# A transformer block on one core: another order of the Down products and another pipeline of the attention's scores

## The chip, the core and the metric

The kernel runs on one core of a Trainium2 chip. The metric is the time of one launch in microseconds on the device. Five engines work side by side and meet at semaphores: TensorE (PE: matmuls, and PEld: its weight loads), VectorE (DVE), ScalarE (ACT), GpSimd (POOL) and SyncE (SP), whose queue issues nearly all transfers. Each engine takes its instructions strictly in the order in which they stand in its own queue.

## The reference

The input x is 4 x 1024 x 512. It goes through a layer norm, and the result `xn` into two branches that are added to x:

```python
h = rmsnorm(xn, qkv_norm_w)
q, k, v = h @ ternary(qkv_w).T          # 16 heads of 32
# linear attention with decay, in chunks of 128 rows; S is a 32x32 state per head
scores = einsum('bhtd,bhsd,hts->bhts', qi, ki, mask)
intra  = einsum('bhts,bhsd->bhtd', scores, vi)
cross  = einsum('bhtd,ht,bhde->bhte', qi, lam_t, S)
o      = scale * (intra + cross)
S      = lam_T * S + einsum('bhtd,ht,bhte->bhde', ki, lam_rev, vi)
out    = rmsnorm(o, norm_w, 1e-06)
att    = rmsnorm(out, proj_norm_w, eps) @ ternary(proj_w).T
ffn    = (silu(xn @ w_gate.T) * (xn @ w_up.T)) @ w_down.T     # hidden 2048
y      = x + att + ffn
```

## The kernel before, in words

**Numbers.** Every float32 operand is split into a high and a low float16 part, and a product is made of two or three float16 products in the same PSUM bank. A split costs an ACT copy (high part) and a subtraction on DVE or POOL (low part).

**Blocks and steps.** The 4096 rows are taken in eight blocks of 512. The FFN of a block is a Python generator; each `yield` of it is one step, and the main loop advances the attention by one step of its own between two FFN steps. So PE's order is: one FFN piece (12 matmuls of 512 columns, or 24 of 256), one attention piece, one FFN piece, and so on. PE's order is the program's (`keep_in_program_order`). A planner with a cost model orders the other engines and the SP queue when the kernel is built, and gives out the buffers of the pools; what it decided stands fixed in each queue.

**FFN.** `ffn_up` makes for hidden tile j the gate product (ACT takes its silu, L716, to `sl`) and the up product (DVE multiplies, L719, to `gf`). From block 2 on, `summed` (L736) takes tiles in pairs: POOL forms differences and sums of their halves (L753 for an even j; L758, L759 and L762 for an odd one), and `split` (L742) splits them: "a" tiles 0 and 1 from the even j, "a" tiles 2 and 3 from the odd j, three "s" tiles from both. The low parts of "a" are POOL's, but for the last pair of a half, where they are DVE's (L746). After eight j, `ffn_seven` (L802) does Down with seven products instead of eight, each a sum over the four pairs, in the order of `SEVEN` (L787), with three PSUM banks. Each entry of `SEVEN` names the tile, the weight row, the bank, whether it begins the bank anew, and the quarters of the output to which DVE then adds the bank (L817). `down_sums` (L824) makes the sums of Down's weights that the seven products need, once, in blocks 1 and 2; their work tile is `ss`, one buffer, which `summed` uses too.

**Attention.** `att_half(b, half)` takes 256 rows, two chunks `u0` and `u1` of 128. There are sixteen such halves; `at` (L986) holds the step at which each starts, 21.5 steps apart in the middle and 14 apart for the last three. Its steps are: q and k in four groups of 16 matmuls of 256 columns (L491), v (L517), two empty steps, then for each chunk four times `scores` and `intra` (four heads each), `cross`, `state`, `norms`, `turn`, `proj`.

- `scores`: 4 matmuls into a bank of `ps_s` (two banks); DVE multiplies with the mask in place (L558), ACT copies the high part (L560), DVE subtracts to the low part (L561).
- `intra`: 8 matmuls with those two as weights. It stands two attention steps after its `scores`, since the two chunks alternate.
- `cross`: 16 matmuls with the state, DVE multiplies to `oc` (L585), POOL adds it to `o` (L586).
- `state`: 12 matmuls; POOL multiplies S with its decay (L598), DVE adds the product in four pieces (L605), ACT and DVE make three float16 copies.
- `norms`: squares on ACT (L616, L619), a product on POOL (L618), nine small DVE operations (L623 to L633) and two POOL powers (L627, L632) for both chunks together; then `o3` on DVE (L636), its split on ACT and POOL (L639, L640), and a transposing DMA (L642).
- `proj`: 8 matmuls on the transposed tiles; DVE adds to the output (L850).

q, k, v, `intra`, `cross`, `state` and `proj` share the three banks of `ps_a`. The buffers that matter are `t32` (512 float32 columns, eight buffers) and `t16` (eleven). In the last half no DMA transposes: `turn` does it on PE (L652) and the two chunks' norms stand apart (`last_half`).

Of the kernel before, what the change touches and what calls it, by code (L numbers as in the profile page):

```python
# [10 lines left out]
F16 = mybir.dt.float16  # L11
# [6 lines left out]
P = 128  # L18
# [10 lines left out]
def block_kernel(ctx, tc, x, qkv_w, qkv_nwT, proj_w, proj_nwT, proj_nw, norm_w, s, w_gu, w_down, out):  # L29
# [95 lines left out]
    def t32():  # L125
        return wt([P, 512], F32, "t32", 8)

# [343 lines left out]
    def att_half(b, half):  # L471
        _, h, rs = blk[b]
        hhi, hlo = h[:, 0], h[:, 1]
        g0 = b * 4 + half * 2
        last_half = g0 == B * N // P - 2

# [35 lines left out]
        for k in range(2):  # L512
# [22 lines left out]
            else:  # L535
                vrs.append(None)
            yield
        class Chunk:
            pass

        cs = []
        for k in range(2):
            u = Chunk()
            u.kn, u.vr = kn[:, :, :, k, :], vrs[k]
            u.g = g0 + k
            u.first = u.g % (N // P) == 0
# [4 lines left out]
            u.pa = None  # L551
            cs.append(u)

        def scores(u, qd):
            pss = bank(ps_s, (P, 4, P))
            for hq in range(4):
                T.matmul(pss[:, hq, :], kst[: 3 * D, hq, qd, u.tsl], qst[: 3 * D, hq, qd, u.tsl], start=True, stop=True)
            V.scalar_tensor_tensor(pss, pss, u.rk, mask[:, 4 * qd : 4 * qd + 4, :], ALU.mult, ALU.mult)  # L558
            u.smh, u.sml = v3(t16()), v3(t16())
            A.copy(u.smh, pss)  # L560
            V.tensor_tensor(u.sml, pss, u.smh, ALU.subtract)  # L561

        def intra(u, qd):
            if qd == 0:
                u.o = t32()
            if qd % 2 == 0:
                u.pa = bank(ps_a, (P, 8, 2, D))
            for hq in range(4):
                h = 4 * qd + hq
                pa = u.pa[:, h % 8].rearrange("p a d -> p (a d)")  # L570
                T.matmul(pa, u.smh[:, hq, :], u.vhl[:, h].rearrange("p a d -> p (a d)"), start=True, stop=False)
                T.matmul(pa[:, :D], u.sml[:, hq, :], u.vhl[:, h, 0, :], start=False, stop=True)
            if qd % 2:
                oh = u.o.rearrange("p (h d) -> p h d", d=D)[:, 4 * qd - 4 : 4 * qd + 4, :]
                A.copy(oh, u.pa[:, :, 1, :])
                V.tensor_tensor(oh, u.pa[:, :, 0, :], oh, ALU.add)  # L576

        def cross(u):
            if u.first:
                return  # L580
            px = bank(ps_a, (P, H, D))
            for h in range(H):
                T.matmul(px[:, h, :], qst[: 3 * D, h % 4, h // 4, u.tsl], Sst[:, h, :], start=True, stop=True)
            oc = t32()
            V.tensor_tensor(oc.rearrange("p (h d) -> p h d", d=D), px, lamt, ALU.mult)  # L585
            G.tensor_tensor(u.o, u.o, oc, ALU.add)  # L586

# [21 lines left out]

        def norms(us):  # L610
            n = len(us)
            k0 = half * 2 + us[0].g - g0
            sq = wt([P, 2, n], F32, f"sq{n}")
            o2s = []
            for i, u in enumerate(us):
                A.activation(junk, u.o, AF.Square, accum_out=sq[:, 0, i : i + 1])  # L616
                o2 = t32()
                G.tensor_tensor(o2, u.o, nw_bc, ALU.mult)  # L618
                A.activation(junk, o2, AF.Square, accum_out=sq[:, 1, i : i + 1])  # L619
                o2s.append(o2)  # L620
            f = wt([P, 4, n], F32, f"f{n}")
            c1, r, r2, e = (f[:, i, :] for i in range(4))
# [11 lines left out]
            for i, u in enumerate(us):  # L634
                u.o3 = t32()
                V.scalar_tensor_tensor(u.o3, o2s[i], e[:, i : i + 1], pnw_bc, ALU.mult, ALU.mult)  # L636
                if u.g < B * N // P - 2:
                    on = wt([P, 2 * C], F16, "vhl", 5).rearrange("p (a c) -> p a c", a=2)
                    A.copy(on[:, 0, :], u.o3)  # L639
                    G.tensor_tensor(on[:, 1, :], u.o3, on[:, 0, :], ALU.subtract)  # L640
                    oT = wt([P, 2 * C], F16, "vhl", 5).rearrange("p (a c t) -> p a c t", a=2, t=P)
                    SY.dma_start_transpose(  # L642
                        oT.rearrange("p a c t -> p (a c) t"), on.rearrange("p a c -> p (a c)")
                    )
                    u.oh, u.ol = oT[:, 0], oT[:, 1]

# [10 lines left out]
        def proj(u):  # L657
# [4 lines left out]
            add_acc(u.g, pp, spp)  # L662

        u0, u1 = cs
        yield
        yield
        scores(u0, 0)
        yield
        scores(u1, 0)
        yield  # L670
        for qd in range(1, 4):
            for u in cs:
                intra(u, qd - 1)
                scores(u, qd)
                yield
        intra(u0, 3)
        cross(u0)
        if last_half:
            norms([u0])
        yield  # L680
        intra(u1, 3)
        yield
        state(u0)
        yield
        yield
        cross(u1)
        norms([u1] if last_half else cs)
        turn(u0)
        yield
        if not u1.last:  # L690
            state(u1)
        yield
        if last_half:
            proj(u0)
        yield
        yield
        turn(u1)
        yield
        if not last_half:
            proj(u0)  # L700
        yield
# [34 lines left out]
    def summed(ops, late):  # L736
# [11 lines left out]
        def done(j, gf):  # L748
# [6 lines left out]
            else:  # L755
                ss = wt([P, 2 * C], F32, "ss", 1)
                f0 = g0[0]
                G.tensor_tensor(ss[:, :UT], gf[:, UT:], f0[:, UT:], ALU.subtract)  # L758
                G.tensor_tensor(ss[:, UT : 2 * UT], ss[:, :UT], f0[:, :UT], ALU.add)  # L759
                split(ops[-1][0][:, 2:], gf, E)  # L760
                split(ops[-1][1][:, :2], ss[:, : 2 * UT], V)
                G.tensor_tensor(ss[:, 2 * UT : 3 * UT], gf[:, :UT], ss[:, :UT], ALU.subtract)  # L762
                split(ops[-1][1][:, 2:3], ss[:, 2 * UT : 3 * UT], V)

        return done

    def ffn_down(b, k, g0, gts, c):
# [56 lines left out]
    def down_sums(g):  # L824

        hh, i = divmod(g, NG // 2)
        w = wt([P, 2, 2, UT], F32, "ss", 1)
        SY.dma_start(w, w_down[2 * g * P : 2 * g * P + 2 * P, :].rearrange("(r p) (f q) -> p r f q", p=P, q=UT))
        for (r, f), (ra, fa), (rb, fb) in (
# [4 lines left out]
        ):  # L834
            G.tensor_tensor(w[:, r, f, :], w[:, ra, fa, :], w[:, rb, fb, :], ALU.subtract)
        o = om[:, g, 2:3]
        for r in range(2):
            t = wt([P, 2 * C], F16, "xn2", 2).rearrange("p (f n q) -> p f n q", f=2, n=2)
            A.activation(t[:, :, 0, :], w[:, r], AF.Copy, scale=o)
            V.scalar_tensor_tensor(t[:, :, 1, :], w[:, r], o, t[:, :, 0, :], ALU.mult, ALU.subtract)  # L840
            SY.dma_start(wd_d[:, hh, 3 + 2 * r : 5 + 2 * r, i].rearrange("p f n q -> p f (n q)"), t.rearrange("p f n q -> p f (n q)"))
# [16 lines left out]
    def load_acc(b):  # L858
        for k in range(2):
            g = 4 * b + 2 * k  # L860
            acc[g // 2] = wt([P, 2, C], F32, "acc", 4)
            SY.dma_start(acc[g // 2], xf[g * P : (g + 2) * P, :].rearrange("(n p) c -> p n c", p=P))
            parts[g] = parts[g + 1] = 1 + (NG if b == 0 else 2 if b == 1 else 8)

# [128 lines left out]
    for b in range(NB):  # L993
        lns = iter(())
        TS = steps[b]
        for i, _ in enumerate(ffn(b) if b else ffn0()):
# [15 lines left out]
            if t == 6 * NG - 6:  # L1012
                SY.dma_start(pnw_bc, proj_nw.partition_broadcast(P))
            if b + 1 < NB:
                if i == TS - (22 if b else 15):
# [62 lines left out]
```

## Time and profile before

| | |
|---|---|
| median of 3 runs | 1374.3 us (1371.63 to 1375.47) |
| profiled execution, its own time | 1374.05 us |
| its span, first to last instruction | 1372.3 us |
| mean granted TensorE clock | 0.989 |
| PE busy | 1306.0 us (95%), 9378 matmuls |
| DVE busy | 893.9 us (65%) |
| ACT busy | 610.2 us (44%) |
| POOL busy | 641.8 us (47%) |
| largest group: gate and up products (L74 psf<-xT,gu), 3072 matmuls | 705.0 us |

How to read the lines. "A <- B: 6.8, 3, 2.9" in the view of waits says that engine line A sat idle 6.8 us in total, 3 times, at most 2.9 us, until B ended. In the timeline a row is a start, a duration, an engine, a source line, the operation, output<-input, shapes and a count; a bracket at its end is the idle time ahead of it and what ended that. PEclk is the share of full TensorE clock that the throttle granted. All matmul helpers have the line L74, so PE's work is told apart by its tiles: psf is the FFN, psa and pss the attention.

### The profile page before, as it was taken

The numbers are of one execution on the slowest core, as the hardware profiler recorded it, in microseconds if no ns is written. First come the engines' busy times: TensorE is split into PE (matmuls) and PEld (weight loads), VectorE is DVE, ScalarE is ACT, GpSimd is POOL, SyncE is SP. The second block draws the span as 40 slices with busy tenths as digits, with TensorE's granted clock in tenths as the row PEclk, the third lists the DMA queues.
The fourth block names the chain that finished last, engine by engine and source line by source line (L and its number), as shares of the span: only waits on it lengthen the run. The fifth ranks groups of instructions, "written<-read, shape, count | busy, mean of one in ns | idle before, by whom it ended". The sixth has DMA issues, their size and how long they took to land.

```text
span 1372.3 us, 23971 instructions
## 1 busy us (share of the span) xinstructions
PE 1306.0 (95%) x9378; PEld 782.9 (57%) x9378; DVE 893.9 (65%) x1599; ACT 610.2 (44%) x1173; POOL 641.8 (47%) x681
## 2 busy tenths in 40 slices
PE   5998999999998999999999999999999999997997
PEld 2443445455556565575757657475665757555645
DVE  7797776654657577665767466575656666557575
ACT  6764554343443435434443354443444254343352
POOL 3757646241453545535463355444554345343352
PEclk9999999999999999999999999999999999998999
DMA  9845756438376583847774656747573747645432
GB/s 342 317 142 169 216 164 205 118 94 215 122 193 212 141 238 99 224 124 201 199 183 142 169 141 187 196 137 208 137 214 117 191 148 164 190 126 137 142 73 77
DMA packets 180689, 233.84 MB, mean 170 GB/s; under 512 B 103264, under 2 KB 113504, under 8 KB 180576
## 3 DMA queue, kind: packets, MB, share of 16 engines
q1 hardware_dynamic: 180432, 232.31, 59.1%
q8 instruction: 73, 1.20, 0.4%
q14 instruction: 40, 0.33, 0.1%
q10 hardware_dynamic: 144, 0.01, 0.0%
HBM read 167.78 MB, written 40.89 MB: 152 GB/s over the span
## 4 chain that ended last, share of the span: by engine, by line
PE 65%; DVE 12%; DMA 10%; POOL 7%; ACT 4%; issue 3%; SPq 1%; POOLq 0%; ACTq 0%; DVEq 0%
PE psf L74 48%; PE psa L74 15%; DMA xin<-in_x_dram 3%; DMA xT<-xn 2%; PE pss L74 2%; DMA vhl<-vhl 1%; DVE t L719 1%; DMA ss<-in_w_down_dram 1%; DVE wda L746 1%; DVE st L396 1%; POOL xn L450 1%; DMA wd_d<-xn 1%; DVE pss L558 1%; DVE t L561 1%; DVE Sst L607 1%
## 5 line engine op out<-in xcount | busy, mean ns | idle before, releaser
L74 PE MATMUL psf<-xT,gu 128*128 128x512 f16 x3072 | 705.0, 382 | 12.5 <-POOL gu L367 4.9
L74 PEld LDWEIGHTS <-gu 128*128 128x128 f16 x3072 | 295.9, 98 | 342.9 <-issue 16.1
L74 PE MATMUL psf<-wdb,ghl 128*128 128x256 f16 (+1 forms) x1344 | 184.4, 294 | 15.3 <-ACT ghl L745 6.8
L74 PEld LDWEIGHTS <-ghl 128*128 128x128 f16 x1536 | 150.4, 100 | 75.1 <-ACT ghl L745 7.7
L560 ACT CAST t<-pss 128x512 f16<-128x512 f32 x128 | 74.7, 585 | 123.0 <-DVE pss L558 121.8
L719 DVE SCALAR_TENSOR_TENSOR t<-psf,bsc,t 128x512 f32<-128x512 f32 x128 | 95.3, 747 | 51.1 <-PE psf L74 36.5
L74 PE MATMUL psa<-h,wqkT 128*128 128x256 f16 x1024 | 122.2, 273 | 1.6 <-DVE t L585 1.6
L716 ACT ACTIVATE t<-psf,ug 128x512 f32<-128x512 f32 x128 | 87.6, 684 | 69.3 <-PE psf L74 68.9
L561 DVE TENSOR_TENSOR t<-pss,t 128x512 f16<-128x512 f32 x128 | 87.9, 687 | 41.5 <-ACT t L560 41.2
L74 PEld LDWEIGHTS <-wqkT 128*128 128x128 f16 x1024 | 99.6, 98 | 21.6 <-issue 1.8
L558 DVE SCALAR_TENSOR_TENSOR pss<-pss,rs,mask 128x512 f32<-128x512 f32 x128 | 96.1, 751 | 14.5 <-PE pss L74 14.1
L745 ACT CAST ghl<-t 128x512 f16<-128x512 f32 x96 | 59.2, 618 | 96.8 <-DVE t L719 55.6
L74 PE MATMUL psf<-wdb,wda 128*128 128x256 f16 x864 | 100.0, 272 | 0.1
L746 DVE TENSOR_TENSOR wda<-ss,wda 128x512 f16<-128x512 f32 x96 | 75.0, 805 | 32.7 <-ACT wda L745 32.0
L533 POOL TENSOR_TENSOR t<-t,t 128x512 f16<-128x512 f32 x28 | 32.8, 1172 | 135.6 <-ACT t L532 135.5
L746 POOL TENSOR_TENSOR ghl<-t,ghl 128x512 f16<-128x512 f32 x72 | 84.2, 1171 | 23.5 <-ACT ghl L745 23.5
L74 PEld LDWEIGHTS <-wda 128*128 128x128 f16 x864 | 83.4, 98 | 9.8 <-issue 0.3
L817 DVE SCALAR_TENSOR_TENSOR acc<-psf,c,acc 128x512 f32<-128x512 f32 x96 | 70.3, 743 | 27.6 <-PE psf L74 27.1
L758 POOL TENSOR_TENSOR ss<-t,t 128x256 f32<-128x256 f32 x48 | 35.8, 746 | 109.8 <-DVE t L719 108.7
L586 POOL TENSOR_TENSOR t<-t,t 128x512 f32<-128x512 f32 x28 | 37.7, 1345 | 90.0 <-DVE t L576 75.3
L753 POOL TENSOR_TENSOR t<-t 128x256 f32<-128x256 f32 x48 | 36.3, 756 | 92.8 <-DVE t L719 92.8
L74 PEld LDWEIGHTS <-t 128*128 128x128 f16 x1040 | 47.7, 97 | 33.1 <-DVE t L561 6.8
(210 smaller groups left out, 1825.2 us busy)
## 6 DMA issues: line engine op xcount, KB each, us to landing
gu<-gu_d SPq DMA_DIRECT2D x112, 512.0 KB, 3.7
wdb<-wd_d SPq DMA_DIRECT2D x84, 512.0 KB, 3.9
qst<-sd SPq DMA_DIRECT2D x48, 256.0 KB, 5.3
kst<-sd SPq DMA_DIRECT2D x48, 256.0 KB, 4.6
xin<-in_x_dram SPq DMA_DIRECT2D x32, 256.0 KB, 4.3
acc<-in_x_dram SPq DMA_DIRECT2D x16, 512.0 KB, 3.9
gu_d<-gu SPq DMA_DIRECT2D x16, 512.0 KB, 4.5
sd<-qhl SPq DMA_DIRECT2D x16, 512.0 KB, 3.1
```

The lines of the kernel that those rows point to most:

```text
L74: tc.keep_in_program_order(nc.tensor.matmul(*a, **k))
L558: V.scalar_tensor_tensor(pss, pss, u.rk, mask[:, 4 * qd : 4 * qd + 4, :], ALU.mult, ALU.mult)
L560: A.copy(u.smh, pss)
L561: V.tensor_tensor(u.sml, pss, u.smh, ALU.subtract)
L586: G.tensor_tensor(u.o, u.o, oc, ALU.add)
L716: pa = A.activation(sl, pm, AF.Silu, scale=ug[:, j // 2 : j // 2 + 1])
L719: pv = V.scalar_tensor_tensor(gf, pm, bs[:, j // 2 : j // 2 + 1], sl, ALU.mult, ALU.mult)
L745: A.copy(dst[:, :, 0, :], src)
L746: E.tensor_tensor(dst[:, :, 1, :], src, dst[:, :, 0, :], ALU.subtract)
L753: G.tensor_tensor(gf[:, UT:], gf[:, :UT], gf[:, UT:], ALU.subtract)
L758: G.tensor_tensor(ss[:, :UT], gf[:, UT:], f0[:, UT:], ALU.subtract)
L817: V.scalar_tensor_tensor(a, pd, c, a, ALU.mult, ALU.add)
```

## The change

It has two parts.

1. `SEVEN` has a new order: the two tiles of the even j first (a0, a1), then those of the odd j (a2, a3), then s1, s0, s2. Tile s0 now adds to three quarters instead of one, and a1 to one instead of two: nine additions on DVE a half instead of eight.
2. The attention: `scores` stands four steps ahead of its `intra`. The masked scores go to a `t32` tile in SBUF, so that the bank is free after one DVE operation, and the low part is POOL's. `cross(u0)` and `state(u0)` stand at the first two score steps, `cross(u1)` and `state(u1)` at the ninth and tenth; `oc` is kept and added to `o` on POOL after the last `intra`. `norms` takes one chunk, and does both norms with one power: four small DVE operations a half (`ek`) and, for each chunk, two additions and a power on POOL replace the nine DVE operations and two powers. A half ends sooner; `at` goes from 21.5 to 21.1 steps. `t32` has ten buffers; `ss` is gone, `down_sums` uses two `t32` tiles, and `summed` uses `xn2` (two buffers, shared with the layer norm).

```diff
     def t32():
-        return wt([P, 512], F32, "t32", 8)
+        return wt([P, 512], F32, "t32", 10)
...
+        ek = wt([P, 2], F32, "ek")
+        V.tensor_scalar(ek, rs[:, 1, half * 2 : half * 2 + 2], kap, None, ALU.mult)
+        V.reciprocal(ek, ek)
+        V.tensor_scalar(ek, ek, (1e-6 * RMS_EPS) ** 0.5, 1e18, ALU.mult, ALU.min)
+        V.tensor_tensor(ek, ek, ek, ALU.mult)
...
         def scores(u, qd):
...
-            V.scalar_tensor_tensor(pss, pss, u.rk, mask[:, 4 * qd : 4 * qd + 4, :], ALU.mult, ALU.mult)
-            u.smh, u.sml = v3(t16()), v3(t16())
-            A.copy(u.smh, pss)
-            V.tensor_tensor(u.sml, pss, u.smh, ALU.subtract)
+            sm = v3(t32())
+            V.scalar_tensor_tensor(sm, pss, u.rk, mask[:, 4 * qd : 4 * qd + 4, :], ALU.mult, ALU.mult)
+            smh, sml = u.sm[qd] = v3(t16()), v3(t16())
+            A.copy(smh, sm)
+            G.tensor_tensor(sml, sm, smh, ALU.subtract)
...
         def intra(u, qd):
...
+            if qd == 3 and not u.first:
+                G.tensor_tensor(u.o, u.o, u.oc, ALU.add)
 
         def cross(u):
...
-            oc = t32()
-            V.tensor_tensor(oc.rearrange("p (h d) -> p h d", d=D), px, lamt, ALU.mult)
-            G.tensor_tensor(u.o, u.o, oc, ALU.add)
+            u.oc = t32()
+            V.tensor_tensor(u.oc.rearrange("p (h d) -> p h d", d=D), px, lamt, ALU.mult)
...
-        def norms(us):
...
-            V.tensor_scalar(c1, rs[:, 1, k0 : k0 + n], kap, None, ALU.mult)
-            V.tensor_tensor(e, c1, c1, ALU.mult)
-            V.tensor_tensor(r, sq[:, 0, :], e, ALU.mult)
-            V.tensor_scalar(r, r, 1.0 / C, 1e-6, ALU.mult, ALU.add)
-            G.tensor_tensor(r, r, mhalf[:, :n], ALU.pow)
-            V.tensor_tensor(r, r, c1, ALU.mult)
-            V.tensor_tensor(e, r, r, ALU.mult)
-            V.tensor_tensor(r2, sq[:, 1, :], e, ALU.mult)
-            V.tensor_scalar(r2, r2, 1.0 / C, RMS_EPS, ALU.mult, ALU.add)
-            G.tensor_tensor(r2, r2, mhalf[:, :n], ALU.pow)
-            V.scalar_tensor_tensor(e, r2, ps_sc, r, ALU.mult, ALU.mult)
...
+        def norms(u):
...
+            A.activation(junk, o, AF.Square, scale=(RMS_EPS / C) ** 0.5, accum_out=sq[:, 0:1])
+            o2 = t32()
+            G.tensor_tensor(o2, o, nw_bc, ALU.mult)
+            A.activation(junk, o2, AF.Square, scale=(1.0 / C) ** 0.5, accum_out=sq[:, 1:2])
+            f = sq[:, 2:3]
+            G.tensor_tensor(f, sq[:, 0:1], u.ek, ALU.add)
+            G.tensor_tensor(f, f, sq[:, 1:2], ALU.add)
+            G.tensor_tensor(f, f, mhalf[:, :1], ALU.pow)
+            u.o3 = t32()
+            V.scalar_tensor_tensor(u.o3, o2, f, pnw_bc, ALU.mult, ALU.mult)
...
+        order = [(u, qd) for qd in range(4) for u in cs]
+        yield
+        yield
+        for i in range(len(order) + 4):
+            if i >= 4:
+                intra(*order[i - 4])
+            if i < len(order):
+                scores(*order[i])
+            if i in (0, 8):
+                cross(cs[i // 8])
+            if i in (1, 9) and not cs[i // 8].last:
+                state(cs[i // 8])
+            if i >= 10:
+                norms(cs[i - 10])
+            yield
+        yield
         turn(u0)
         yield
...
         turn(u1)
         yield
-        if not last_half:
-            proj(u0)
+        proj(u0)
         yield
         proj(u1)
...
-                ss = wt([P, 2 * C], F32, "ss", 1)
+                ss = wt([P, C], F32, "xn2", 2)
...
+                split(ops[-1][1][:, :2], ss, V)
+                s4 = wt([P, C], F32, "xn2", 2)[:, :UT]
+                G.tensor_tensor(s4, gf[:, :UT], ss[:, :UT], ALU.subtract)
+                split(ops[-1][1][:, 2:3], s4, V)
...
     SEVEN = (
         (("a", 0), 0, 1, True, ((0, 0),)),
-        (("a", 3), 5, 0, True, ((1, 0),)),
+        (("a", 1), 4, 0, True, ((1, 1),)),
         (("a", 2), 1, 2, True, ((0, 0),)),
-        (("s", 0), 6, 1, False, ((0, 1),)),
+        (("a", 3), 5, 0, False, ((1, 0),)),
         (("s", 1), 3, 2, True, ((1, 1),)),
-        (("a", 1), 4, 1, False, ((1, 1), (1, 0))),
+        (("s", 0), 6, 1, False, ((0, 1), (1, 0), (1, 1))),
         (("s", 2), 2, 2, False, ((0, 1),)),
     )
...
     def down_sums(g):
...
-        w = wt([P, 2, 2, UT], F32, "ss", 1)
+        w = [t32(), t32()]
...
-    at = [round(36 + 22.4 * min(n, 4) + 21.5 * max(n - 4, 0)) for n in range(2 * NB - 2)]
+    at = [round(36 + 22.4 * min(n, 4) + 21.1 * max(n - 4, 0)) for n in range(2 * NB - 2)]
```

More of the change, by code (lines that the diff above doesn't have):

```diff
@@ L474, in att_half @@
         g0 = b * 4 + half * 2
-        last_half = g0 == B * N // P - 2
         qst = wt([P, 4, CC, UT], F16, "qst", 1)
@@ L550, in att_half @@
             u.rk = rs[:, 1, half * 2 + k : half * 2 + k + 1]
-            u.pa = None
+            u.ek = ek[:, k : k + 1]
+            u.pa, u.sm = None, {}
             cs.append(u)
@@ L567, in intra @@
                 u.pa = bank(ps_a, (P, 8, 2, D))
+            smh, sml = u.sm.pop(qd)
             for hq in range(4):
@@ L570, in intra @@
                 pa = u.pa[:, h % 8].rearrange("p a d -> p (a d)")
-                T.matmul(pa, u.smh[:, hq, :], u.vhl[:, h].rearrange("p a d -> p (a d)"), start=True, stop=False)
-                T.matmul(pa[:, :D], u.sml[:, hq, :], u.vhl[:, h, 0, :], start=False, stop=True)
+                T.matmul(pa, smh[:, hq, :], u.vhl[:, h].rearrange("p a d -> p (a d)"), start=True, stop=False)
+                T.matmul(pa[:, :D], sml[:, hq, :], u.vhl[:, h, 0, :], start=False, stop=True)
             if qd % 2:
@@ L608, in state @@
             A.activation(Sst[D : 2 * D], S, AF.Copy, scale=STS / VS)
-        def norms(us):
[L611 to L622, printed above, removed]
-            V.tensor_scalar(c1, rs[:, 1, k0 : k0 + n], kap, None, ALU.mult)
-            V.tensor_tensor(e, c1, c1, ALU.mult)
-            V.tensor_tensor(r, sq[:, 0, :], e, ALU.mult)
-            V.tensor_scalar(r, r, 1.0 / C, 1e-6, ALU.mult, ALU.add)
-            G.tensor_tensor(r, r, mhalf[:, :n], ALU.pow)
-            V.tensor_tensor(r, r, c1, ALU.mult)
-            V.tensor_tensor(e, r, r, ALU.mult)
-            V.tensor_tensor(r2, sq[:, 1, :], e, ALU.mult)
-            V.tensor_scalar(r2, r2, 1.0 / C, RMS_EPS, ALU.mult, ALU.add)
-            G.tensor_tensor(r2, r2, mhalf[:, :n], ALU.pow)
-            V.scalar_tensor_tensor(e, r2, ps_sc, r, ALU.mult, ALU.mult)
[L634 to L645, printed above, removed]
@@ new lines, in norms @@
+        def norms(u):
+            o = u.o
+            sq = wt([P, 3], F32, "sq")
+            A.activation(junk, o, AF.Square, scale=(RMS_EPS / C) ** 0.5, accum_out=sq[:, 0:1])
[8 more added lines that the diff above has]
+            V.scalar_tensor_tensor(u.o3, o2, f, pnw_bc, ALU.mult, ALU.mult)
+            if u.g < B * N // P - 2:
+                on = wt([P, 2 * C], F16, "vhl", 5).rearrange("p (a c) -> p a c", a=2)
+                A.copy(on[:, 0, :], u.o3)
+                G.tensor_tensor(on[:, 1, :], u.o3, on[:, 0, :], ALU.subtract)
+                oT = wt([P, 2 * C], F16, "vhl", 5).rearrange("p (a c t) -> p a c t", a=2, t=P)
+                SY.dma_start_transpose(
+                    oT.rearrange("p a c t -> p (a c) t"), on.rearrange("p a c -> p (a c)")
+                )
+                u.oh, u.ol = oT[:, 0], oT[:, 1]
@@ L664, in att_half @@
         u0, u1 = cs
+        order = [(u, qd) for qd in range(4) for u in cs]
         yield
         yield
-        scores(u0, 0)
-        yield
[L669 to L687, printed above, removed]
-        turn(u0)
[L689 to L693, printed above, removed]
-            proj(u0)
-        yield
+        for i in range(len(order) + 4):
[10 more added lines that the diff above has]
+            yield
+        yield
+        turn(u0)
         yield
@@ L698, in att_half @@
         yield
-        if not last_half:
-            proj(u0)
+        proj(u0)
         yield
@@ L826, in down_sums @@
         hh, i = divmod(g, NG // 2)
-        w = wt([P, 2, 2, UT], F32, "ss", 1)
-        SY.dma_start(w, w_down[2 * g * P : 2 * g * P + 2 * P, :].rearrange("(r p) (f q) -> p r f q", p=P, q=UT))
+        w = [t32(), t32()]
+        for r in range(2):
+            SY.dma_start(w[r], w_down[(2 * g + r) * P : (2 * g + r + 1) * P, :])
+        w = [t.rearrange("p (f q) -> p f q", q=UT) for t in w]
         for (r, f), (ra, fa), (rb, fb) in (
@@ L834, in down_sums @@
         ):
-            G.tensor_tensor(w[:, r, f, :], w[:, ra, fa, :], w[:, rb, fb, :], ALU.subtract)
+            G.tensor_tensor(w[r][:, f, :], w[ra][:, fa, :], w[rb][:, fb, :], ALU.subtract)
         o = om[:, g, 2:3]
@@ L838, in down_sums @@
             t = wt([P, 2 * C], F16, "xn2", 2).rearrange("p (f n q) -> p f n q", f=2, n=2)
-            A.activation(t[:, :, 0, :], w[:, r], AF.Copy, scale=o)
-            V.scalar_tensor_tensor(t[:, :, 1, :], w[:, r], o, t[:, :, 0, :], ALU.mult, ALU.subtract)
+            A.activation(t[:, :, 0, :], w[r], AF.Copy, scale=o)
+            V.scalar_tensor_tensor(t[:, :, 1, :], w[r], o, t[:, :, 0, :], ALU.mult, ALU.subtract)
             SY.dma_start(wd_d[:, hh, 3 + 2 * r : 5 + 2 * r, i].rearrange("p f n q -> p f (n q)"), t.rearrange("p f n q -> p f (n q)"))
@@ L862, in load_acc @@
             SY.dma_start(acc[g // 2], xf[g * P : (g + 2) * P, :].rearrange("(n p) c -> p n c", p=P))
-            parts[g] = parts[g + 1] = 1 + (NG if b == 0 else 2 if b == 1 else 8)
+            parts[g] = parts[g + 1] = 1 + (NG if b == 0 else 2 if b == 1 else 2 * (4 + k))
     def ffn(b):
@@ L1013, in block_kernel @@
                 SY.dma_start(pnw_bc, proj_nw.partition_broadcast(P))
+                V.tensor_scalar(pnw_bc, pnw_bc, ps_sc, None, ALU.mult)
             if b + 1 < NB:
```

3 lines of the change are left out of this document (removed).

## The prediction, made before the run

> **What bounds the kernel now.** I read the engine totals of the page first, then the chain, PE's waits, and the timeline around the waits that the edits touch.
>
> ```profile
> span 1372.3 us, 23971 instructions
> PE 1306.0 (95%) x9378; PEld 782.9 (57%) x9378; DVE 893.9 (65%) x1599; ACT 610.2 (44%) x1173; POOL 641.8 (47%) x681
> ```
>
> PE is busy in 1306.0 of 1372.3 us, and the change leaves its 9378 matmuls as they are. So it can win only the 66.3 us in which PE sits idle, and the time by which a slower clock stretches matmuls. The profiled execution took 1374.05 us, 1.75 more than its span and 0.25 under the median of the runs, 1374.3; I add to 1374.05. PE's waits:
>
> ```profile
> PE psa L78 <- DVE xin L415: 9.1, 3, 8.3
> PE psf L74 <- ACT ghl L745: 6.8, 3, 2.9
> PE psa L74 <- DMA vhl<-vhl: 5.6, 5, 2.7
> ...
> PE psa L74 <- DVE t L561: 4.7, 7, 1.8
> ...
> PE psf L74 <- DVE ghl L746: 4.6, 3, 3.5
> PE psf L74 <- DVE acc L817: 3.2, 3, 2.0
> ...
> PE pss L74 <- DMA qst<-sd: 2.6, 2, 2.1
> ...
> PE psa L74 <- DVE t L585: 1.6, 2, 0.8
> ...
> PE psa L74 <- ACT t L560: 1.4, 1, 1.4
> ```
>
> The edits reach L745 and L746 (11.4), L560 and L561 (6.1), vhl (5.6), qst (2.6), L585 (1.6) and two small waits of the last `turn` (1.0): 28.3 us. The rest, xin above all, lies mostly in the first 140 us, or belongs to edges that stay.
>
> **A. The order of SEVEN.** The last pair's split before Down, as the timeline has it:
>
> ```profile
> 1246.29 0.73 DVE L719 SCALAR_TENSOR_TENSOR t<-psf,bsc,t 128x512 f32<-128x512 f32 x1
> 1246.94 3.07 DVE L469 SCALAR_TENSOR_TENSOR h<-t,nwT,h 128x256 f16<-128x256 f32 x4
> ...
> 1247.05 0.62 ACT L745 CAST ghl<-t 128x512 f16<-128x512 f32 x1
> 1247.73 0.39 PE L74 MATMUL psf<-wdb,ghl 128*128 128x256 f16 x2 [2.92 <-ACT ghl L745]
> 1250.53 1.03 DVE L746 TENSOR_TENSOR ghl<-t,ghl 128x512 f16<-128x512 f32 x1
> 1251.63 2.95 PE L74 MATMUL psf<-wdb,ghl 128*128 128x256 f16 x13 [3.51 <-DVE ghl L746]
> ```
>
> Tile a3 is Down's second product, and its high part ends 2.9 us and its low part 6.4 us after PE wanted them. With a1 second, the odd j's first tile (a2) is third, one product of 24 matmuls, 2.62 us, later. The three places have gaps of 1.78 (at 414), 6.43 (here) and 3.28 (1346), 11.5 in all with the small ones. The first goes; the second leaves 3.8, most of it the four L469 operations, 3.07 us, which DVE has queued ahead of L746 here and which the change moves too; the third leaves 0.7. I take 1.5 us left and a gain of 9.9; bounds 7.0 (2.62, 2.62 and 1.78 alone) and 11.4. Twelve more L817 additions are 12 x 0.743 = 8.9 us of DVE, hidden behind its 478 idle us; s0's three follow in one go, 2.2 us, while s2's product keeps PE for 2.6.
>
> **B. Scores four steps ahead.** Today PE catches up with the chain:
>
> ```profile
> 258.33 0.59 ACT L560 CAST t<-pss 128x512 f16<-128x512 f32 x1 [2.47 <-DVE pss L558]
> ...
> 258.97 0.20 PE L74 MATMUL psa<-vhl,t 128*128 128x64 f16 x1 [1.37 <-ACT t L560]
> 259.69 0.45 PE L74 MATMUL psa<-vhl,t 128*128 128x32 f16 x7 [0.52 <-DVE t L561]
> ```
>
> The new chain is L558 0.75 + L560 0.59 + a POOL subtraction, for which I take L746's and L640's 1.16: 2.5 us. The lead is four attention steps of 3.03 us (1323.98 to 1327.01), 12.1 us, so the slack is 9.6. Gain: all 6.1; the lower bound is 3. DVE loses 128 x 0.687 = 87.9 us here and 52.5 of small norm operations; with the additions of A it falls to some 770. POOL gains 128 x 1.16 = 148 and some 7 of powers and additions: 797, 59%. In the worst stretch, four steps that hold an odd j, POOL has 4 x 1.16 and 5.4 for `summed` (0.76 + 2 x 1.17 + 0.75 + 0.83 + 0.74): 10.0 of 12.1 us. It fits, but without much room.
>
> Which of the two engines may be slowed is seen in L746's rows (ns, min/median/max):
>
> ```profile
> L746 DVE TENSOR_TENSOR wda<-ss,wda x96: 407/692/3006, 369.8 to 1349.0; 128x512 f16<-128x512 f32 x48, 128x256 f16<-128x256 f32 x48
> L746 POOL TENSOR_TENSOR ghl<-t,ghl x72: 1147/1157/1409, 362.3 to 1328.3; 128x512 f16<-128x512 f32 x72
> ```
>
> POOL's subtraction hardly varies; DVE's stretches to 3.0 us. So I hold POOL at 1.16 and let DVE pay: with 148 us more of POOL, some 11% of the span, and about 244 two-input DVE operations, at most 15 us of DVE time, hidden in its idle time. [...]
>
> **C. Norms by the chunk.** The chain from the last `intra(u0)` to `proj(u0)` becomes: eviction 0.37 + 0.42, `oc` 1.35, L618 1.31, second square 0.82, additions and power 2 x 0.23 + 0.55, o3 0.77, split 0.62 + 1.16, transposes 5.4: 13.2 us, with nine starts of about 0.2 some 15 to 16. PE does five FFN pieces (13.1), an `intra` (0.45) and two q or k groups (3.8) in between: 17.3. Today five waits are 5.6 us; I take a gain of 2.6, bounds 5.6 and -6 (16 halves a little late). Where the cover goes, each half pays its lateness in full. The addition of `oc` now waits on POOL for the last eviction (0.37 + 0.42 after PE); behind it stand only `summed` operations, which feed tiles that Down wants some steps later. The transposes stay two to a half on SP's queue, now one by one, with the loads of wdb behind each; these are asked for over a step ahead, and I cost that at nothing, 1.2 us a transpose if that cover is gone (L642's issue on SP). `down_sums` issues one more load in each of its eight calls and no longer shares a buffer with `summed`; its products come blocks later, so nothing again, and its waits on w_down leave the path of POOL's work.
>
> **D. Cross and state early; the last three halves.** The waits on qst (2.6) and L585 (1.6) go, as `cross(u1)` frees qst and its bank six steps earlier. New: 14 steps apart, the next half's k product stands right after `state(u1)` and takes the bank that L605's additions must empty, and these wait for POOL's S x decay (L598, 1.05). In the first such place POOL has the tail of an odd j ahead of it (0.95 left of gf, 3.5 of `summed`, then 1.05 and four additions of 0.28: 6.6 us, less 0.9 of PE work = 5.7); in the second three low parts (3.55 - 0.89 = 2.7). Together -8.4, net -4.2; bounds -9 and -1. No row of before shows this wait, so the lower end stays in the range.
>
> **E. The tail.** `turn` and `proj` of the last half stand as elsewhere (1.0 us of waits); two last transfers of 256 KB leave instead of one of 512. I take +0.5; bounds -1 and 1.5.
>
> **F. The clock.**
>
> ```profile
> 1000.00:1020.00 20.00, 17.25 (x126) 12.02 (x124) 11.87 (x28) 9.68 (x16) 10.07 (x14) 1.00 0.65 161
> 1240.00:1260.00 20.00, 13.57 (x93) 9.75 (x91) 15.05 (x24) 6.56 (x13) 7.95 (x9) 0.76 0.43 111
> ```
>
> (The number before the last two is the granted clock.) After gaps of 2.06 (1239), 6.4 (1250) and 1.37 + 0.52 (259) PE ran at half clock for some 3.4 us each; after 2.75 at 1015 it did not. With two or three of these gone I win 5.2 us, each place giving half of 3.4; a stall of 5.7 us in D costs 3 again: +2, bounds 0 and 5. [...]
>
> **G. Unseen waits** in a new order of every queue: -3, bounds 0 and -8 (the size of L745's or L561's group).
>
> Sum: 9.9 + 6.1 + 2.6 - 4.2 + 0.5 + 2 - 3 = 13.9; 1374.05 - 13.9 = 1360.
>
> **The rivals.**
> - *POOL becomes late* (slower). Low parts stand in POOL's queue behind `summed` and behind S x decay, which wait for DVE and PE. If POOL lags over the 9.6 us of B in a half, `intra` waits for a whole chain, 2.5 us. Against the 13.9, six halves use up the gain; with eight of the sixteen it is 1374.05 - 13.9 + 20.2 = 1380, with all 1401. For it: 10.0 of 12.1 in a stretch. Against: 59% on the whole, and a lag has all even stretches to recover. 0.18.
> - *Waits form anew*: C at its lower bound -6 instead of 2.6 and G at -8: 1374.05 - 0.3 = 1374; with half of that 1367. I say 1367 to 1379: PE has to be fed by something, and the next engine may be as late. 0.16.
> - *All works*: D at -1, C 5.6, F 5, G 0: 9.9 + 6.1 + 5.6 - 1 + 0.5 + 5 = 26.1, or 1348; 1345 to 1350. 0.10.
> - *The forecast*, 1350 to 1367: 0.56.
>
> **How the numbers follow.** 0.3%, 4.1 us, is about what a measurement of this kernel can tell from no change: 1370.2 to 1378.4. Faster: 0.56 + 0.10 + 0.05 of the second rival; same 0.09 of it; slower 0.18 + 0.02. The range, 1346 to 1376, leaves out the first rival and little else.
>
> **What would show it.** In the changed profile: L745 and L746 under 2 us among PE's waits, L560 and its POOL successor at none, vhl under 4, a new psa wait on DVE's S additions of 3 to 9 us near the last three halves, POOL near 797 us, DVE near 770, full clock around Down. I am wrong if `intra` waits on POOL in the middle halves, if `proj` waits in most halves, or if the first 140 us change.

## The result, and the profile after

The changed kernel takes 1380.16 us (median of 14 runs) against 1374.32 for the kernel before (14 runs): ratio 1.0036, 95% interval 1.0019 to 1.0054. It is 0.36% slower; 1360 was forecast, 14 us faster. The profiled execution took 1380.81 us, its span is 6.7 longer than before.

Lines are named by the changed kernel from here on: L700 silu, L703 the up product, L586 the addition of `oc`, L625 and L628 the two squares, L627 the product with `nw`, L634 `o3`, L637 and L638 its split, L730 the low parts of tiles, L614 the additions to S. The page's totals:

```profile
span 1379.0 us, 23944 instructions
PE 1307.0 (95%) x9378; PEld 783.0 (57%) x9378; DVE 839.2 (61%) x1395; ACT 615.3 (45%) x1173; POOL 803.4 (58%) x871
PE 55%; DVE 13%; POOL 11%; DMA 10%; ACT 4%; issue 4%; SPq 2%; POOLq 0%; DVEq 0%; ACTq 0%
```

PE's busy time has moved by 1.0 us, its idle time from 66.3 to 72.0. The third line, the engines' shares of the chain that ended last, had PE 65% and POOL 7% before: more of the chain now runs through POOL. PE's waits (us in total, times, longest):

```profile
PE psf L74 <- ACT t L700: 14.5, 8, 4.8
...
PE psf L74 <- DVE t L703: 8.5, 7, 3.3
...
PE psf L74 <- DVE acc L802: 4.9, 5, 1.8
...
PE psa L74 <- DVE S L614: 3.6, 2, 2.3
PE psa L74 <- DMA vhl<-vhl: 2.5, 1, 2.5
PE psf L74 <- DVE ghl L716: 2.3, 1, 2.3
...
PE psf L74 <- ACT ghl L729: 1.6, 1, 1.6
...
PE psa L74 <- DVE t L595: 1.3, 1, 1.3
...
PE psf L74 <- DVE ghl L730: 1.0, 1, 1.0
```

Nearly all that the change was to remove is gone: no score operation is in the list any more (6.1 before), the last pair's split in `summed` (L729, L730) has 2.6 left of 11.4, the transposed tiles 2.5 of 5.6. In its place PE waits for the FFN's own evictions, the operations that read a psf bank out of PSUM and so free it: 23.0 us on silu and the up product, where the kernel before (its L716 and L719) had 4.0:

```profile
PE psf L74 <- DVE t L719: 3.1, 2, 1.9
...
PE psf L74 <- ACT t L716: 0.9, 3, 0.3
```

Of the 23.0 us, 18.5 stand at six places from 288 us on, each in a stretch of the norms; the rest is before 210 us. The longest of these waits in the timeline:

```profile
369.03 1.15 POOL L730 TENSOR_TENSOR ghl<-t,ghl 128x512 f16<-128x512 f32 x1
370.14 1.26 POOL L586 TENSOR_TENSOR t<-t,t 128x512 f32<-128x512 f32 x1
371.36 0.73 POOL L743 TENSOR_TENSOR xn<-xn,t 128x256 f32<-128x256 f32 x1
371.43 0.63 ACT L625 ACTIVATE junk<-t 128x512 f16<-128x512 f32 x1 [2.98 <-POOL t L586]
...
372.73 1.26 POOL L586 TENSOR_TENSOR t<-t,t 128x512 f32<-128x512 f32 x1
373.95 1.71 POOL L627 TENSOR_TENSOR t<-t,nw_bc 128x512 f32<-128x512 f32 x1
...
375.69 0.63 ACT L628 ACTIVATE junk<-t 128x512 f16<-128x512 f32 x1 [2.48 <-POOL t L627]
...
377.07 0.67 ACT L700 ACTIVATE t<-psf,ug 128x512 f32<-128x512 f32 x1
...
377.79 2.72 PE L74 MATMUL psf<-xT,gu 128*128 128x512 f16 x6 [4.83 <-ACT t L700]
```

In these rows POOL works without a break and does `oc` of both chunks, the odd tile's sums and the product with `nw`. ACT has both squares of the first chunk and the first square of the second ahead of silu in its queue, and stands idle 2.98 and 2.48 us for POOL; silu comes late, and PE waits 4.83 us for a bank. At 703 the same happens (L628 and L637 ahead of silu, 2.97 us), and at 288 the up product stands in DVE's queue behind a stretched L827 (3.67 us; the median of its 16 is 0.75) and behind `o3` (1.89 us), which waits for POOL's power.

### The profile page after: what moved, and what is told of

Its sections match the earlier page's. It is cut to its first block, busy times and chain, and to the rows that moved or that the text cites. A ratio compares the mean times of both kernels' runs of the same rounds, so it can differ in the third digit from the quotient of the medians.

```text
span 1379.0 us, 23944 instructions
## 1 busy us (share of the span) xinstructions
PE 1307.0 (95%) x9378; PEld 783.0 (57%) x9378; DVE 839.2 (61%) x1395; ACT 615.3 (45%) x1173; POOL 803.4 (58%) x871
## 4 chain that ended last, share of the span: by engine, by line
PE 55%; DVE 13%; POOL 11%; DMA 10%; ACT 4%; issue 4%; SPq 2%; POOLq 0%; DVEq 0%; ACTq 0%
PE psf L74 40%; PE psa L74 14%; DMA xin<-in_x_dram 2%; PE pss L74 2%; DMA t<-in_w_down_dram 2%; DVE wda L730 1%; DVE t L703 1%; POOL t L627 1%; POOL t L586 1%; DVE h L469 1%; DVE t L565 1%; DMA kst<-sd 1%; POOL xn L450 1%; DVE acc L802 1%; POOL t L568 1%
## 5 line engine op out<-in xcount | busy, mean ns | idle before, releaser
L74 PEld LDWEIGHTS <-gu 128*128 128x128 f16 x3072 | 295.6, 98 | 364.9 <-issue 36.2
L568 POOL TENSOR_TENSOR t<-t,t 128x512 f16<-128x512 f32 x128 | 154.7, 1213 | 87.2 <-ACT t L567 84.0
L567 ACT CAST t<-t 128x512 f16<-128x512 f32 x128 | 78.9, 617 | 133.2 <-DVE t L565 130.0
L703 DVE SCALAR_TENSOR_TENSOR t<-psf,bsc,t 128x512 f32<-128x512 f32 x128 | 95.3, 746 | 59.1 <-PE psf L74 53.9
L700 ACT ACTIVATE t<-psf,ug 128x512 f32<-128x512 f32 x128 | 86.9, 682 | 64.3 <-PE psf L74 63.7
L565 DVE SCALAR_TENSOR_TENSOR t<-pss,rs,mask 128x512 f32<-128x512 f32 x128 | 94.8, 742 | 32.6 <-PE pss L74 32.5
L730 DVE TENSOR_TENSOR wda<-xn,wda 128x512 f16<-128x512 f32 x96 | 92.2, 988 | 32.9 <-ACT wda L729 32.2
L729 ACT CAST ghl<-t 128x512 f16<-128x512 f32 x96 | 58.9, 616 | 102.4 <-POOL t L737 53.7
L802 DVE SCALAR_TENSOR_TENSOR acc<-psf,c,acc 128x512 f32<-128x512 f32 x108 | 78.4, 744 | 40.3 <-PE psf L74 40.0
L730 POOL TENSOR_TENSOR ghl<-t,ghl 128x512 f16<-128x512 f32 x72 | 85.8, 1192 | 9.6 <-ACT ghl L729 9.6
L532 POOL TENSOR_TENSOR t<-t,t 128x512 f16<-128x512 f32 x28 | 32.7, 1169 | 89.6 <-ACT t L531 89.6
L742 POOL TENSOR_TENSOR xn<-t,t 128x256 f32<-128x256 f32 x48 | 36.8, 766 | 60.5 <-DVE t L703 60.0
L729 ACT CAST wda<-xn 128x512 f16<-128x512 f32 x96 | 48.3, 510 | 48.7 <-POOL xn L743 44.8
```

The lines of the kernel that those rows point to most:

```text
L74: tc.keep_in_program_order(nc.tensor.matmul(*a, **k))
L532: G.tensor_tensor(vrl, vr, vrh, ALU.subtract)
L565: V.scalar_tensor_tensor(sm, pss, u.rk, mask[:, 4 * qd : 4 * qd + 4, :], ALU.mult, ALU.mult)
L567: A.copy(smh, sm)
L568: G.tensor_tensor(sml, sm, smh, ALU.subtract)
L700: pa = A.activation(sl, pm, AF.Silu, scale=ug[:, j // 2 : j // 2 + 1])
```

## The experiments

Each ratio is to the kernel before as measured in the same series (medians of 1374.3 to 1375.5 us); medians of two series can differ by a microsecond on that account alone.

The first theory after the result was that POOL carries too much in the stretch of the norms, and that what stands behind the norms in the queues of ACT and DVE, silu and the up product, pays. Rivals: POOL's load on the whole (the low parts of the scores); the form of the norms, one chunk at a time; the queue order alone.

**Each part of the change by itself.** `down_only` is the kernel before with the new SEVEN; `att_only` the changed kernel with the old one.

```diff
-        (("a", 3), 5, 0, True, ((1, 0),)),
+        (("a", 1), 4, 0, True, ((1, 1),)),
...
-        (("a", 1), 4, 1, False, ((1, 1), (1, 0))),
+        (("s", 0), 6, 1, False, ((0, 1), (1, 0), (1, 1))),
```

> The kernel before with the new order of SEVEN alone. If term A is real by itself: the waits on the last pair's split (11.4 us before) shrink to 2 to 4, and the time falls by 6 to 10 us, to 1364 to 1368. If the split only moves the wait to the eviction of the banks (s0's three additions) the time stays within 1371 to 1377.

> The changed kernel with the old order of SEVEN. If the two parts add up: slower than the changed kernel by what the Down order gains, 6 to 10 us, so 1386 to 1390, with some 23 us of PE waits on the evictions of gate and up products (L700, L703) as in the changed kernel. If the new Down order is what makes those evictions late: 1365 to 1374 and those waits under 8 us.

Measured: 1373.75 us, ratio 0.9980 (0.9965 to 0.9995), and 1387.88 us, ratio 1.0081 (1.0058 to 1.0103). So the attention is what costs, some 11 us, and `att_only` has 21.6 us of waits on silu and the up product. The Down order gains: some 6 us in the changed kernel (1.0081 against 1.0036; 7.7 by the medians of the two series), but only 2.7 in the kernel before. There the split's wait shrank, and the evictions' grew (lines of the kernel before, PE's waits of `down_only`):

```profile
PE psf L74 <- DVE t L719: 7.0, 6, 2.0
PE psf L74 <- DVE ghl L746: 5.8, 3, 4.2
...
PE psf L74 <- ACT t L716: 2.8, 4, 1.8
```

L745 and L746 together fell from 11.4 to 6.5 (L745 has 0.7 left, L746 itself rose from 4.6 to 5.8), and L716 and L719 rose from 4.0 to 9.8. The time is in the range of the second expectation, but not for its reason: the wait on L817, where s0's additions are, fell from 3.2 to 0.5.

**POOL's load on the whole.** `low_on_dve` takes the scores' low parts from POOL.

```diff
-            G.tensor_tensor(sml, sm, smh, ALU.subtract)
+            V.tensor_tensor(sml, sm, smh, ALU.subtract)
```

> The changed kernel with the low part of the scores on DVE as before (L568), 128 operations and 155 us less on POOL. Theory POOL load (POOL is the late engine in the stretch of the norms, because it carries the low parts too): PE's waits on L700 and L703 fall from 23 to under 10 us and the time to 1362 to 1370. Theory norms by the chunk (the chain over ACT, POOL and DVE is laid into two steps, and silu and the up product stand behind it, whatever POOL's load): the waits stay at 18 us or more and the time within 1375 to 1385.

Measured: 1380.29 us, ratio 1.0034 (1.0019 to 1.0049), no different from the changed kernel. POOL is down from 803.4 to 663.9 us, and the waits stay:

```profile
PE psf L74 <- ACT t L700: 14.6, 7, 5.2
...
PE psf L74 <- DVE t L703: 8.2, 6, 3.3
```

The low parts on POOL are not the cause of these waits: the stretch shown above holds none of them, and the waits stay with the low parts gone. The time is a weaker proof, since the run shifts the work and doesn't remove it: DVE rises from 839.2 to 893.2 us, 108.1 of it the low parts. POOL's mean load says nothing of the waits here.

**The form of the norms.** `norms_before` does both chunks' norms together after the last `intra`, with two powers and the small operations on DVE.

```diff
-            if i >= 10:
-                norms(cs[i - 10])
+            if i == 11:
+                norms(cs)
```

> The changed kernel with the norms as before: both chunks together after the last intra, two powers and the small operations on DVE. Theory norms by the chunk: PE's waits on L700 and the up product fall from 23 to under 10 us, the time to 1362 to 1370. Theory POOL load: the waits stay at 18 us or more, the transposed tiles come later still (vhl waits over 5 us), and the time is 1378 to 1390.

Measured: 1419.27 us, ratio 1.0316 (1.0293 to 1.0340).

```profile
PE psa L74 <- DMA vhl<-vhl: 36.2, 12, 5.6
PE psf L74 <- ACT t L704: 12.4, 8, 5.4
```

The form by the chunk is right for this pipeline: with the old one `proj` waits 36.2 us for its tiles. Silu's waits stay at 12.4 with the old form too, but the up product's (L707) go from 8.5 to 1.1. Together they are 13.5, between what the two expectations said (under 10, 18 or more). So the form by the chunk may have a part in the up product's waits, or PE, held up by `proj`, no longer meets them; that is not shown. Neither expectation foresaw so late a `proj`.

**The additions of `oc`.** `oc_on_dve` lets the `oc` tile be `o`, to which DVE adds each half of the `intra` bank straight from PSUM; for this `cross(u1)` comes four steps earlier. L586's 28 POOL additions and 56 of ACT's copies go.

```diff
-                A.copy(oh, u.pa[:, :, 1, :])
-                V.tensor_tensor(oh, u.pa[:, :, 0, :], oh, ALU.add)
-            if qd == 3 and not u.first:
-                G.tensor_tensor(u.o, u.o, u.oc, ALU.add)
+                if u.first:
+                    A.copy(oh, u.pa[:, :, 1, :])
+                else:
+                    V.tensor_tensor(oh, u.pa[:, :, 1, :], oh, ALU.add)
+                V.tensor_tensor(oh, u.pa[:, :, 0, :], oh, ALU.add)
...
-            if i in (0, 8):
-                cross(cs[i // 8])
+            if i in (0, 4):
+                cross(cs[i // 4])
```

> The changed kernel with the state's part oc added on DVE as PSUM is read (cross(u1) four steps earlier, L586's 28 POOL additions of 1.26 us and 56 of ACT's L583 copies gone). Theory POOL in the norms' stretch (two oc additions, two products L627 and two low parts L638 meet the odd tile's sums there, some 13 us of POOL in 9): L700 and L703 waits fall from 23 to 8 to 15 us, the time to 1368 to 1375. Theory order only (the planner has laid the squares and o3's split ahead of silu, whatever POOL does): waits 18 us or more, 1377 to 1384.

Measured: 1357.95 us, ratio 0.9873 (0.9861 to 0.9886): 22 us less than the changed kernel and 1.3% less than the kernel before. PE's waits and, in the timeline, the same norms (its lines are one higher):

```profile
PE psf L74 <- ACT t L701: 5.3, 6, 2.4
...
PE psf L74 <- DVE t L704: 3.2, 5, 1.1
```

```profile
366.06 0.41 DVE L587 TENSOR_TENSOR t<-psa,t 128x256 f32<-128x256 f32 x1
...
366.50 0.63 ACT L626 ACTIVATE junk<-t 128x512 f16<-128x512 f32 x1 [1.10 <-DVE t L587]
...
367.11 1.27 POOL L628 TENSOR_TENSOR t<-t,nw_bc 128x512 f32<-128x512 f32 x1
...
368.42 0.63 ACT L629 ACTIVATE junk<-t 128x512 f16<-128x512 f32 x1 [1.19 <-POOL t L628]
...
370.93 0.68 ACT L701 ACTIVATE t<-psf,ug 128x512 f32<-128x512 f32 x1
...
371.66 2.53 PE L74 MATMUL psf<-xT,gu 128*128 128x512 f16 x11 [1.11 <-ACT t L701]
```

The first square follows the eviction at once; ACT's idle times are 1.10 and 1.19 instead of 2.98 and 2.48, and PE's is 1.11 instead of 4.83. Of the span's 22.0 us, 14.5 are these two rows (23.0 to 8.5) and 8.2 PE's busy time (1307.0 to 1298.8; mean granted clock 0.988 to 0.993): the gaps are fewer and the clock is higher. Other rows cost 0.7 more. The time is below both expectations, which had no term for the clock. How much of the 8.2 the gaps account for is not certain: `low_on_dve`, with the same waits on the evictions as the changed kernel, has 1303.5 us of busy time.

This edit does three things, so two controls take them apart. `cross_early` has the earlier `cross(u1)` alone; `oc_pool_idle_add` is `oc_on_dve` with 28 additions on POOL that nothing reads, where L586 stood.

```diff
+            if qd == 3 and not u.first:
+                G.tensor_tensor(t16(), u.o, nw_bc, ALU.add)
```

> The changed kernel with cross(u1) four steps earlier and nothing else: the part of oc_on_dve that isn't the addition. If POOL's two additions at the norms are the cause: no better than the changed kernel, 1377 to 1383, L700 and L703 waits still about 20 us. If the early cross gave the gain: 1358 to 1366.

> oc_on_dve with 28 additions that nothing reads put back on POOL where L586 stood (last intra, ahead of the product with nw). The output is unchanged; POOL's queue in the norms' stretch is as long as in the changed kernel. Theory POOL's queue there: 1370 to 1382, waits of gate and up products on silu and the up product back to 15 us or more. If it was the link in the chain or ACT's copies and not POOL's time: 1356 to 1364.

Measured: 1380.40 us, ratio 1.0052 (1.0031 to 1.0073), and 1385.94 us, ratio 1.0081 (1.0055 to 1.0107). The early cross is worth nothing; additions without a reader take the whole gain back, and 5.8 us more than that by the medians. So POOL's time at that place is enough to cost the gain, and neither the loss of ACT's copies, which are gone here too, nor the early cross gave it by itself. PE's waits of `oc_pool_idle_add` (lines three higher):

```profile
PE psf L74 <- ACT t L703: 9.2, 6, 3.7
...
PE psf L74 <- DVE acc L805: 8.0, 4, 3.5
PE psf L74 <- DVE t L706: 6.5, 6, 3.5
```

By the waits the return is less complete. The evictions are back at 15.7 us, half of the way from 8.5 to 23.0: the stalls at 288 and 378 us are there again (3.55 and 3.69 us), the one at 703 hardly (0.47 instead of 2.97). So a part of those waits may belong to the link in the chain, the sum that the first square has to wait for. Of the 25.2 us of span above `oc_on_dve`, 7.2 are the evictions, 9.2 PE's busy time (1308.0), 3.5 the last pair's split, 3.3 the transfer of xT and 1.5 L805; why the last three came up isn't shown. The added operation also takes a `t16` buffer, which no run tests by itself.

**The queue order.** `staged_pin` writes each chunk's norms in three stages, a step apart, the later two behind the last silu and up product already written. `ek_four` gives `ek` four buffers instead of two. `pin_oc_ek` has both and `oc` on DVE.

```diff
+            yield
+            with after(list(pin)):
+                A.activation(junk, o2, AF.Square, scale=(1.0 / C) ** 0.5, accum_out=sq[:, 1:2])
...
-        ek = wt([P, 2], F32, "ek")
+        ek = wt([P, 2], F32, "ek", 4)
```

> The changed kernel with each chunk's norms written in three stages, one step apart, the second and third held behind the last silu and up product already written. Same operations, same buffers. Theory order only: where a silu now stands ahead, its wait goes (377.8 us: 4.8; 703.4: 3.0; about half of the 23 us), time 1366 to 1375, with vhl waits up by 2 to 6. Theory POOL in the norms' stretch: the chain itself is late, what silu wins proj loses, 1376 to 1384.

> The changed kernel with four buffers of ek instead of two, so that DVE's small operations on it wait for no POOL read of an earlier half. If these waits (8.7 us on DVE, one ahead of the up product at 1246.8) cost the PE: 2 to 5 us less, 1375 to 1378. If they lie beside the norms' chain anyway: within 1378 to 1382.

> The three edits together (oc on DVE, norms in three stages behind silu, four buffers of ek). If both causes hold: 1358 to 1368, under the kernel before. If the evictions are late for another reason: 1372 or more.

Measured: 1401.56 us, ratio 1.0188 (1.0172 to 1.0205); 1381.33 us, ratio 1.0042 (1.0027 to 1.0056); 1369.80 us, ratio 0.9955 (0.9941 to 0.9969). PE's waits of `staged_pin`:

```profile
PE psa L74 <- DMA vhl<-vhl: 28.5, 9, 5.5
...
PE psf L74 <- ACT t L712: 2.5, 2, 2.2
PE psf L74 <- DVE t L715: 2.2, 3, 1.2
```

The order works as meant, 23.0 us on evictions become 4.7, but the norms then come late and `proj` waits 28.5 instead of 2.5, so that the time is above both expectations. Order alone chooses who pays here; shortening the work, as in `oc_on_dve`, is what gained. `ek`'s waits lie beside others and cost nothing that can be measured. `pin_oc_ek` loses 12 us against `oc_on_dve`, 9.1 of them on vhl (12.5 against 3.4).

**Further on from there.** `oc_low_dve` also puts `o3`'s low part (L638) on DVE; `oc_state5` has `state(u1)` right behind the early `cross(u1)`.

```diff
-                G.tensor_tensor(on[:, 1, :], u.o3, on[:, 0, :], ALU.subtract)
+                V.tensor_tensor(on[:, 1, :], u.o3, on[:, 0, :], ALU.subtract)
...
-            if i in (1, 9) and not cs[i // 8].last:
-                state(cs[i // 8])
+            if i in (1, 5) and not cs[i // 4].last:
+                state(cs[i // 4])
```

> oc_on_dve with the low part of o3 (L638 of the changed kernel, 30 operations of 1.16 us) on DVE too. If POOL's queue at the norms still limits: 2 to 6 us less than oc_on_dve, 1352 to 1356. If POOL has slack there now and DVE's two-input operations meet POOL's: 1357 to 1363.

> oc_on_dve with state(u1) right after the early cross(u1), four steps earlier. The k product behind state(u1) in the last halves, which waited 3.6 us for S's additions, then waits no more: 1353 to 1357. If POOL's S x decay comes in the way of the low parts of the scores: intra waits on POOL appear and it is 1358 or more.

Measured: 1365.02 us, ratio 0.9935 (0.9916 to 0.9954), and 1356.94 us, ratio 0.9870 (0.9844 to 0.9896). With L638 on DVE the evictions' waits fall on (8.5 to 6.1), but it is 7 us slower than `oc_on_dve`, which neither expectation allowed. In the two profiles 3.7 us of this are PE's busy time and the rest is 1 us or so each on several waits; the cause stays open. So less POOL work in the stretch of the norms (741.8 us in all against 770.2) is not a gain by itself. `oc_state5` rids PE of the wait on S (3.6), and no wait of `intra` on POOL appears, but a new one of 3.5 us on `cross`'s eviction takes its place; its time can't be told from that of `oc_on_dve`. `oc_on_dve` and `oc_state5` are the fastest versions, both 1.3% under the kernel before.

## Why the prediction was wrong

By the steps of the prediction, from PE's waits before and after:

- **A** (9.9): the split's waits went from 11.4 to 2.6, 8.8 us, though a wait of 2.3 on the split of block 1 (L716) is new. As a time it is worth some 6 in the new pipeline and 2.7 in the old. In the old one L716 and L719 of that kernel grew by 5.8 as the split's waits fell, and the prediction had no term for that.
- **B** (6.1): exact; the chain of 2.5 us hides behind the four steps, and POOL's 803.4 us is near the 797. (DVE's 839.2 is not near the 770; see the last section.)
- **C** (2.6): 3.1. How narrow the cover is, was right as well: `norms_before` and `staged_pin` fall off it with 36.2 and 28.5 us. The 0.2 us of its nine starts was the author's estimate; where nothing else stands ahead, the trace of before has 0.03 to 0.08 (L586 ends at 1354.15, L616 and L618 start at 1354.18 and 1354.23).
- **D** (-4.2): about -1.2. The wait on S was forecast as 8.4 and is 3.6. S's product waits only for the copies of `state(u0)`, and POOL has it done at 1204, 23 us ahead; only L614's four additions are left (1.17), at the second place behind three of L802 (2.07):

```profile
1226.81 0.83 PE L74 MATMUL psa<-t,kn 128*128 128x128 f16 x12
1227.67 1.17 DVE L614 TENSOR_TENSOR S<-S,psa 32x128 f32<-32x128 f32 x4
1227.69 0.72 POOL L742 TENSOR_TENSOR xn<-t,t 128x256 f32<-128x256 f32 x1 [5.04 <-DVE t L703]
1228.89 1.38 PE L74 MATMUL psa<-h,wqkT 128*128 128x256 f16 x11 [1.26 <-DVE S L614]
```

- **E** (+0.5) was about right. **F** (+2): -1.0, since there is half clock behind new gaps too: behind the three longest waits the granted clock is 0.78 (288 to 295 us; 0.50 from 287.6 to 291.0), 0.56 (377 to 384) and 0.66 (703 to 708; 0.50 from 704.0 to 707.4). `oc_on_dve`, with those gaps gone or short, has a clock of 1.00 from 362 to 374 us, where the changed kernel's longest wait was, and 8.2 us less of PE's busy time.
- **G, the step that failed**: "Unseen waits in a new order of every queue: -3, bounds 0 and -8". It is -23.4: 19.0 on silu and the up product, 1.5 on L802, 2.3 on L716, 1.9 on wdb, 1.4 on issue, less 2.7 on rows that the change doesn't touch (xin, gm, gu, xT).

A to F sum to 16.4 by their measured waits (8.8 + 6.1 + 3.1 - 1.2 + 0.6 - 1.0), against 16.9 forecast, by luck in part: D came out 3.0 us better than forecast and F 3.0 worse. With G that is -7.0, and the span grew by 6.7. So the time failed in G, and it was not unforeseeable. The prediction counted POOL's load in the stretch of the scores (10.0 of 12.1 us) and not in that of the norms, though step C had listed the operations: for each chunk `oc` 1.35, the product 1.31, 1.0 of small ones and the low part 1.16, for two chunks in two steps (6.1 us at 3.03) 9.6 us, and an odd tile's sums on top. And it costed a late chain by who reads it (`proj`), not by what is queued behind it. Step C says of the addition of `oc` that "behind it stand only `summed` operations": that holds at most for POOL's queue. On ACT and DVE silu and the up product stand behind the links that wait, and they feed PE at every step. In `oc_on_dve` 14.5 of the 19.0 us go with the additions of `oc`, their time and their link together.

The first rival, "POOL becomes late", came out at the measured time, 1380, but by the wrong road. It put the lateness on the low parts and the wait on `intra`; there is no such wait, and with the low parts off POOL (`low_on_dve`) the stalls stay. That the number fits is luck. Two of the signs by which the prediction would have called itself wrong, `intra` waiting on POOL and `proj` waiting in most halves, did not come up: both look at the readers of the chain.

## What to carry to other kernels

Cost a chain that hops between engines twice: once for its reader, and once for everything that stands behind each waiting link in a strict queue; here it was evictions that free PSUM banks, and PE paid at once (4.83 us at 378, 23.0 in all). Count an engine's load in the stretch where the chain runs, not on the whole: 140 us moved from POOL to DVE elsewhere changed nothing, while 33 us less POOL work, 28 additions at that place, went with 22 us of time. It is no rule that less is better: `oc_low_dve` took more off POOL there and was slower than `oc_on_dve`. To learn whether an operation costs by its time or by its result, put one back that nothing reads, and compare the waits too, not only the time.

## What was not expected of the hardware

DVE paid more for POOL's work than the 15 us allowed. The group of the high-low split of the s tiles, by form, in the kernel before, in the changed one and in `low_on_dve` (count, then busy us and mean ns of one):

```profile
L746 DVE TENSOR_TENSOR wda<-ss,wda 128x512 f16<-128x512 f32 x48 | 47.5, 989 | 32.3 <-ACT wda L745 31.8
```

```profile
L730 DVE TENSOR_TENSOR wda<-xn,wda 128x512 f16<-128x512 f32 x48 | 54.2, 1129 | 31.5 <-ACT wda L729 31.1
```

```profile
L730 DVE TENSOR_TENSOR wda<-xn,wda 128x512 f16<-128x512 f32 x48 | 38.0, 792 | 25.9 <-ACT wda L729 25.6
```

The same DVE operation takes 989, 1129 and 792 ns, and POOL's total (641.8, 803.4 and 663.9 us) does not order them. What does is how many of the 48 meet POOL in time. In the three traces 13, 9 and 19 of them overlap no POOL operation, and every one of these takes 670 to 694 ns. Those over 0.9 us number 15, 24 and 6, the longest takes 3.0 us, and POOL is busy for 85 to 95% of their time. The kernel before's L561, a DVE subtraction of the same shape that reads one input from PSUM, is not stretched: 51 of its 128 overlap POOL, and none takes over 693 ns.

With its other forms the splits went from 95.8 to 121.0 us. DVE came to 839 us where 770 was forecast: 25 of this are the splits, some 22 other two-input operations that stretch (busy us before and after: `o3` 23.5 and 31.7, L469 43.5 and 50.2, L827 12.7 and 17.6, L616 20.6 and 22.9), and the four `ek` operations take 28.7, for which the forecast's sum (893.9 - 87.9 - 52.5 + 8.9 = 762) leaves 8. POOL isn't spared either: its score operation has a mean of 1213 ns, where L746's on POOL had 1171 before (the medians are 1156 and 1157), and the product with `nw` went from a mean of 1307 to 1455 ns. So both engines stretch here, DVE's splits by more: 14% on the mean of the s tiles' split (989 to 1129 ns), POOL's product with `nw` 11%. The splits' stretch did not set the time: `oc_on_dve` has nearly the same (1165 ns) and is the faster by 22 us.
